# 48 list entries of each block fetched as single rows by SP and ScalarE beside the gathers of GpSimd

## The chip, the cores and the metric

The kernel runs on one core of a Trainium2 chip. The time is the device time of one execution in microseconds; a run's time is set against the median of three runs of the kernel before.

## The reference, cut to what matters

A graph layer with 50,000 nodes of 128 float32 numbers and 1,650,000 edges, sorted by destination; 50,000 of them lead from a node to itself.

```python
Xs = X[src]
m_data = Xs @ W_data.T + b_data
m_ctrl = Xs @ W_control.T + b_control
msg = jnp.where((edge_types == 0)[:, None], m_data, m_ctrl)
agg = jax.ops.segment_sum(msg, dst, num_segments=X.shape[0])
out = agg + (X @ W_self.T + b_self)
x = layernorm(x + relu(out))
```

## The kernel before

Since the matrices are applied after the sum, the kernel sums rows of x for each node and edge type and multiplies afterwards. The work goes by blocks of the sorted list. A block covers at most B = 124 nodes and has Q = 2 steps; a step has R = 14 chunks of P = 128 list entries. For each chunk GpSimd (POOL) issues one indirect DMA ("gather", line 507) that fetches 128 rows of x into one slice of a slot `y`; five slots (SLOTS) of 14 chunks go round. TensorE (PE) waits for a step's 14 gathers at once (line 514) and multiplies each chunk with a 0/1 matrix `oh` of 128 columns (64 nodes of a window, two edge types), which adds the rows into `acc` in PSUM (line 530). A float32 product is two matmul passes in the trace.

VectorE (DVE) makes these matrices for a block two blocks ahead (AHEAD = 2): `oh` at line 482, the counts of rows `cnt` for the bias at line 490. It adds `acc` into the running sums of a block (line 539), makes the moments of the rows and the result `o` (line 604). ScalarE (ACT) takes the square root for two blocks at a time (line 595). SP loads the list for ten blocks at a time (lines 182 and 184), windows of transposed x for eight (`xw`, its position read into registers at line 458) and stores each block's 124 rows (line 609), whose address is in a register.

An edge from a node to itself needs no gather: its row is in the transposed x that is loaded anyway. So 53 more list entries of each step (F; with LATE = 10 handed on, 63 columns) take the places of such edges in the list. `fill` (lines 363 to 392) does this on DVE up to five blocks ahead: it finds the places (`m`, line 372), puts in the new entries (`new`, `v_new`, lines 375 and 379), makes the list of row numbers `idx` that the gathers read (line 383), and finds the columns that were left out (`old`, `by`, lines 388 and 391). `columns` (lines 270 to 353) prepares ten blocks' lists.

The order on every engine is the order in which the program is written; each engine works through its own in turn and waits where a semaphore says so. The loop over blocks is in lines 662 to 726. In the middle of a block, after the first 7 products of a step, PE does a small product (line 398) for which DVE's `fill` waits (line 370). The block numbers come from these lines; the first block (and the last) take no fills ("plain"), and the last holds what remains of the list:

```python
CE = Q * SIZE
BE = CE + Q * F
NBLK = 2 + (E + LATE - CE) // BE
REST = E + LATE - CE - (NBLK - 2) * BE
```

So there are 448 blocks, 446 of them with 3,690 entries; the last has 686 entries in 6 chunks.

Of the kernel before, what the change touches and what calls it, by code (L numbers as in the profile page):

```python
# [11 lines left out]
F32 = mybir.dt.float32  # L12
BF16 = mybir.dt.bfloat16
U8 = mybir.dt.uint8
I32 = mybir.dt.int32
AF = mybir.ActivationFunctionType
ALU = mybir.AluOpType
AX = mybir.AxisListType
SP = mybir.EngineType.SP
DVE = mybir.EngineType.DVE  # L20

N = 50000
D = 128
ROW = 4 * D
E = 1650000
P = 128
# [6 lines left out]
R = 14  # L33
W = 64
Q = 2
# [3 lines left out]
F = 53  # L39
LATE = 10  # L40
FX = LATE + F
R1 = R
H = R + 1
C1 = Q * R1
SIZES = [P] * R
SIZE = sum(SIZES)
CE = Q * SIZE
BE = CE + Q * F
NBLK = 2 + (E + LATE - CE) // BE
REST = E + LATE - CE - (NBLK - 2) * BE  # L50
REST_ROWS = [min(n, max(0, REST - q * SIZE - sum(SIZES[:r]))) for q in range(Q) for r, n in enumerate(SIZES)]
# [2 lines left out]
GB = 10  # L54
GROUPS = -(-NBLK // GB)
GC = GB * C1
AHEAD = 2
SLOTS = 5
RAHEAD = 5
LOOP = 2048.0  # L60
COLS = 256
# [24 lines left out]
def plain(b):  # L86

    return b == 0 or b >= NBLK - 1
# [3 lines left out]
    return bass.AP(tensor=ap.tensor, offset=ap.offset, ap=[[0, n], *ap.ap])  # L92


def straight(ctx, tc, c, x, x_t, edges_t, edges_f, dst_first, first_p, out):

# [13 lines left out]
    eds = ctx.enter_context(tc.tile_pool(name="eds", bufs=2))  # L112
    ohp = ctx.enter_context(tc.tile_pool(name="ohp", bufs=AHEAD + 1))
    gat = ctx.enter_context(tc.tile_pool(name="gat", bufs=SLOTS))
    fil = ctx.enter_context(tc.tile_pool(name="fil", bufs=2))
    stp = ctx.enter_context(tc.tile_pool(name="stp", bufs=3))
    ps = ctx.enter_context(tc.tile_pool(name="ps", bufs=2, space=bass.MemoryType.PSUM))
# [59 lines left out]
    nc.vector.memset(stats, 0.0)  # L177
    most = keep.tile([P, GROUPS], F32, name="most")

    def load_edges(g):  # L180
        t = eds.tile([P, 3, GB, C1], I32, name="sdt", bufs=1)
        nc.sync.dma_start(t.rearrange("p m b c -> p (m b c)"), edges_t[:, g * 3 * GC:(g + 1) * 3 * GC])
        f = eds.tile([GB, 3, Q * FX], I32, name="sdt_f", bufs=1)
        nc.sync.dma_start(f.rearrange("b m f -> b (m f)"), edges_f[g * GB:(g + 1) * GB, :])
        loads[g] = {n: t[:, m] for m, n in enumerate("sdt")} | {n + "f": f[:, m] for m, n in enumerate("sdt")}


# [82 lines left out]
    def columns(g):  # L270

        a = loads.pop(g)
        first = begin[:, g * GB:(g + 1) * GB, :]
        steps = "p b (q r) -> p b q r"

# [87 lines left out]
    def fill(b):  # L363

        if plain(b):
            return
        g, i = divmod(b, GB)
        two = lists[b % 2]
        vf, cb = two[:, :Q * FX], two[:, Q * FX:]
        nc.vector.tensor_copy(cb, cb_g[g][:, i, :])  # L370
        m = fil.tile([P, C1, FX], F32, name="m", bufs=1)
        nc.vector.tensor_tensor(m, rk_g[g][:, i, :, None].to_broadcast([P, C1, FX]),  # L372
                                rank_no_ps[:, None, :].to_broadcast([P, C1, FX]), op=ALU.is_equal)
        new = fil.tile([P, C1, FX], F32, name="new", bufs=1)
        nc.vector.tensor_tensor(new.rearrange("p (q r) f -> p q r f", r=R1), m.rearrange("p (q r) f -> p q r f", r=R1),  # L375
                                vf.rearrange("p (q f) -> p q f", f=FX)[:, :, None, :].to_broadcast([P, Q, R1, FX]),
                                op=ALU.mult)
        v = fil.tile([P, C1], F32, name="v_new")
        nc.vector.tensor_reduce(v, new, AX.X, ALU.add)  # L379
        vi = fil.tile([P, C1], I32, name="vi")  # L380
        nc.vector.tensor_tensor(vi, v, stay_g[g][:, i, :], op=ALU.add)
        idx = fil.tile([P, C1], I32, name="idx", bufs=RAHEAD + 2)
        nc.vector.tensor_single_scalar(idx, vi, COLS.bit_length() - 1, op=ALU.logical_shift_right)
        nc.vector.scalar_tensor_tensor(col_g[g][:, i, :], idx, -float(COLS), vi, op0=ALU.mult, op1=ALU.add)
        idxs[b] = idx

        old = fil.tile([P, C1, FX], F32, name="old", bufs=1)
        nc.vector.tensor_tensor(old, m, cb[:, :, None].to_broadcast([P, C1, FX]), op=ALU.mult)  # L388
        by = fil.tile([P, Q, FX], BF16, name="by")
        with nc.allow_low_precision(reason="whole numbers below 256, one of them not 0"):  # L390
            nc.vector.tensor_reduce(by, old.rearrange("p (q r) f -> p q f r", r=R1), AX.X, ALU.add)  # L391
        bys[b] = by
# [43 lines left out]
    def passes_of(b):  # L436

        of = 2 if b == NBLK - 1 else PASS
        for p in range(C // of):
            q = p * of // R  # L440
            yield q, [k for k in chunks_of(b, q) if k // of == p]
# [44 lines left out]
    def counts(b):  # L486

        cnt = ohp.tile([P, Q, 2 * W], BF16, name="cnt")
        with nc.allow_low_precision(reason="whole numbers up to R1"):
            nc.vector.tensor_reduce(cnt, ohs[b].rearrange("p (q r) w -> p q w r", r=R1), AX.X, ALU.add)  # L490
        cnts[b] = cnt
# [9 lines left out]
    def gathers(b, ks):  # L501
# [13 lines left out]
        tc.declare_fence(wait.ins, group=f"rows{b}_{ks[0]}")  # L515
        return y

    def products(b, q, ks):
        of_step = chunks_of(b, q)
        if b == NBLK - 1:  # L520
            ys[b, q] = gathers(b, ks)
        elif ks[0] == of_step[0]:
            ys[b, q] = gathers(b, of_step)
        y = ys[b, q]
        if ks[0] == 0:
            accs[b] = ps.tile([P, Q, 3, W], F32, name="acc")
        acc = accs[b][:, q]
        for k in ks:
            r = REST_ROWS[k] if b == NBLK - 1 else SIZES[k % R]
            nc.tensor.matmul(acc[:, :2, :].rearrange("p t w -> p (t w)"), y[:r, k % R, :], ohs[b][:r, column(k), :],  # L530
                             start=k == of_step[0], stop=k == of_step[-1])
        if ks[-1] == of_step[-1] and q == steps_of(b)[-1]:
            for t in range(2):
                nc.tensor.matmul(accs[b][:, :q + 1, 2, :], to_row[:, t, :], cnts[b][:, :q + 1, t * W:(t + 1) * W],  # L534
                                 start=t == 0, stop=t == 1)
# [121 lines left out]
    for b in range(1, AHEAD):  # L657
        onehot(b)
        counts(b)
    made, fresh = 2, [2]  # L660
    ready = []
    for b in range(NBLK):
        if b == NBLK - 2:
            find_bad()
        if b == NBLK - 1:
            if pair(b - 2):
                store(pair(b - 2))
                ready.extend(pair(b - 2))
            while ready:
                store_rows(ready.pop(0))  # L670
        if b + 3 < NBLK:
            window(b + 3)
        g, i = divmod(b, GB)
        if i == 0 and g + 1 < GROUPS:
            load_edges(g + 1)
        due, fresh = fresh, range(made + 1, min(b + RAHEAD, made + (2 if b > GB // 2 else 1), NBLK - 1) + 1)
        made += len(fresh)
        for f in fresh:
            spread(f)
        if b > 0:  # L680
            add_all(b - 1)
        begin_sums(b)
        if b == NBLK - 1:
            layer(b - 1)
            moments(b - 1)
            root(pair(b - 1))
            own_part(b)
            store(pair(b - 1))
            for done in pair(b - 1):
                store_rows(done)  # L690
            for step, ks in passes_of(b):
                if ks:
                    products(b, step, ks)
            break
        if b + AHEAD < NBLK:
            onehot(b + AHEAD)
            counts(b + AHEAD)
        for q, (step, ks) in enumerate(passes_of(b)):
            if ks:
                products(b, step, ks)  # L700
            if q == 0:
                for f in due:
                    left_out_columns(f)
                for f in fresh:
                    fill(f)
            if q == 1 and b > 0:
                layer(b - 1)
            if q == 1:
                left_out_numbers(b + 1)
            if q == 1 and b > 0:  # L710
                moments(b - 1)
            if q == 1:
                for f in due:
                    left_out_matrix(f)
            if q == 1 and b + 1 < NBLK:
                positions(b + 1)
                left_out_rows(b + 1)
            if q == 2 and i == GB // 2 - 1 and g + 1 < GROUPS:
                columns(g + 1)
            if q == 1 and b > 1 and pair(b - 2):  # L720
                store(pair(b - 2))
                ready.extend(pair(b - 2))
            if q == 3 and b > 0 and pair(b - 1):
                root(pair(b - 1))
            if q == 3 and ready:
                store_rows(ready.pop(0))
# [231 lines left out]
def gnn_resnorm(  # L958
# [3 lines left out]
    x_t: bass.AP,  # L962
    edges_t: bass.AP,
    edges_f: bass.AP,
    dst_first: bass.AP,
    first_p: bass.AP,
    src: bass.AP,
# [34 lines left out]
             b_data=b_data, b_ctrl=b_ctrl, b_self=b_self)  # L1002

    with ExitStack() as own:
        straight(own, tc, c, x, x_t, edges_t, edges_f, dst_first, first_p, out)
    found = nc.values_load(bad, min_val=0, max_val=4 * P,
                           skip_runtime_bounds_check_because="a count of at most 3 * P + 2")
    with tc.If(found > 0):  # L1008
# [55 lines left out]
```

## Time and profile before

| | |
|---|---|
| median of 3 runs | 15663.81 us (15662.4 to 15665.03) |
| profiled execution | 15668.22 us |
| its span, from the first to the last instruction | 15666.5 us |
| mean granted TensorE clock | 0.664 |
| packets of the DMA engines | 474784, 905.35 MB |

In the profile's groups of instructions a row gives line, engine, operation, the tiles written and read, shapes, the count, then the busy time with the mean of one in ns, and the idle time of the engine just before them with what ended it. In the waits a row gives engine, tile and line, what it waited for, the total in us, how often and the longest. A timeline row gives start, length, engine, line and operation. A row of one line's or tile's instructions gives the least, median and greatest length in ns, and the first and last start in us. A row of windows gives the busy times (and counts) of PE, PE's weight loads, DVE, ACT and POOL, then the clock, the DMA share and GB/s. "POOLq", "SPq" and the like are the sequencers of the engines, which issue DMAs and wait for semaphores. A row of queues gives packets, MB and the share of the time of 16 DMA engines.

### The profile page before, as it was taken

The page shows a single profiled execution, that of the slowest core. Times are in us where ns is not written, and L with a number is a line of the kernel's source. Part 1 is how long each engine was busy: PE and PEld are TensorE (multiplying, and loading weights), DVE is VectorE, ACT ScalarE, POOL GpSimd, SP SyncE. Part 2 cuts the span into 40 slices and gives each one's busy share as a digit, 9 for nine tenths or more (in the row PEclk, how much of TensorE's full clock was granted, in tenths as well). Part 3 has the DMA queues.
Part 4 walks back from the last instruction along what each step waited for, and adds up shares of the span by engine and source line. Part 5 has one row for each costly group of instructions (what it writes and reads, how often), then busy time and mean ns, then how long its engine had stood idle before and what let it go on. Part 6 is the DMA issues. An engine that isn't in the chain of part 4 may idle for free. (4 is left out here: it accounts for less than half of the span.)

```text
span 15666.5 us, 97614 instructions
## 1 busy us (share of the span) xinstructions
PE 5887.6 (38%) x32436; PEld 5492.1 (35%) x32437; DVE 11899.2 (76%) x12418; ACT 69.8 (0%) x231; POOL 11833.4 (76%) x12532
## 2 busy tenths in 40 slices
PE   3333333333333333333333333333333333333333
PEld 3333333333333333333333333333333333333333
DVE  9777777777777777777777777777777777777775
ACT  0000000000000000000000000000000000000000
POOL 7777777777777777777777777777777777777777
PEclk7666666666666666666666666666666666666666
DMA  2222222222222222222222222222222222222222
GB/s 61 59 57 58 57 57 59 57 60 57 57 58 57 59 57 57 59 58 59 57 57 58 57 59 57 58 58 57 58 57 57 58 57 60 57 57 58 57 59 53
DMA packets 474784, 905.35 MB, mean 58 GB/s; under 512 B 204474, under 2 KB 260873, under 8 KB 474271
## 3 DMA queue, kind: packets, MB, share of 16 engines
q0 software_dynamic: 400736, 821.40, 20.7%
q1 hardware_dynamic: 73096, 77.42, 1.7%
q8 instruction: 260, 4.26, 0.1%
q14 instruction: 254, 2.07, 0.0%
q10 hardware_dynamic: 438, 0.20, 0.0%
HBM read 869.76 MB, written 28.44 MB: 57 GB/s over the span
## 5 line engine op out<-in xcount | busy, mean ns | idle before, releaser
L507 POOL DMA_INDIRECT y<-in_x,idx x12516 | 11826.0, 945 | 3813.9 <-issue 3811.3
L530 PE MATMUL acc<-oh,y 128*128 128x128 f32 x25044 | 4965.0, 384 | 9493.2 <-PEq L514 9493.2
L530 PEld LDWEIGHTS acc<-oh,y 128*128 128x128 f32 x25044 | 4754.9, 293 | 9816.0 <-issue 5313.4
L490 DVE TENSOR_REDUCE cnt<-oh 128x256 bf16<-128x3584 f32 x448 | 2763.2, 6168 | 15.4
L482 DVE TENSOR_TENSOR oh<-col,small 128x3584 f32<-128x3584 f32 x448 | 1736.7, 3877 | 0.0
L539 DVE TENSOR_TENSOR sums<-acc,sums 128x192 f32 x895 | 319.7, 357 | 1768.7 <-PE acc L534 1749.8
L391 DVE TENSOR_REDUCE by<-old 128x126 bf16<-128x1764 f32 x446 | 1466.4, 3288 | 15.5
L370 DVE COPY small<-cb 128x28 f32<-128x28 f32 x446 | 84.1, 189 | 1547.8 <-PE small L398 1547.8
L372 DVE TENSOR_TENSOR m<-rk,small 128x1764 f32<-128x1764 f32 x446 | 888.4, 1992 | 15.2
L375 DVE TENSOR_TENSOR new<-m,small 128x1764 f32<-128x1764 f32 x446 | 888.2, 1992 | 15.2
L379 DVE TENSOR_REDUCE v_new<-new 128x28 f32<-128x1764 f32 x446 | 887.9, 1991 | 15.2
L388 DVE TENSOR_TENSOR old<-m,small 128x1764 f32<-128x1764 f32 x446 | 884.6, 1984 | 0.0
L569 PE MATMUL po<-wmsgT,sums 128*124 128x128 f32 x1792 | 315.5, 299 | 0.0
L559 PE MATMUL po<-own_w,xT 128*124 128x256 f32 x896 | 269.4, 382 | 0.8 <-DVE h L575 0.8
L555 DVE TENSOR_TENSOR sums<-pl,sums 128x372 f32<-128x372 f32 x446 | 243.2, 545 | 16.3
L569 PEld LDWEIGHTS po<-wmsgT,sums 128*124 128x124 f32 x1792 | 229.5, 187 | 54.8 <-issue 0.8
L423 DVE TENSOR_TENSOR pl<-pl,xT 128x248 f32<-128x248 f32 x446 | 189.4, 425 | 50.4 <-DVE xT L476 5.1
L567 PE MATMUL po<-bias,sums 3*124 3x128 f32 x896 | 215.1, 319 | 0.8 <-DVE sums L539 0.8
L567 PEld LDWEIGHTS po<-bias,sums 3*124 3x124 f32 x896 | 128.9, 180 | 152.1 <-issue 150.8
L406 DVE TENSOR_SCALAR z<-node_no,at 126x256 bf16<-126x256 f32 x446 | 161.0, 361 | 15.9
L361 PE MATMUL small<-v_f,row_of 74*128 74x126 bf16 x446 | 98.8, 222 | 177.7 <-DVE at L405 128.4
L476 DVE COPY xT<-xw 128x124 f32 x448 | 104.5, 233 | 79.5 <-issue 75.5
(144 smaller groups left out, 2727.9 us busy)
## 6 DMA issues: line engine op xcount, KB each, us to landing
y<-in_x,idx POOLq DMA_INDIRECT x12516
xw<-in_x_t SPq DMA_DIRECT2D x56, 496.0 KB
out<-o SPq DMA_DIRECT2D x448, 62.0 KB
sdt<-in_edges_t SPq DMA_DIRECT2D x45, 420.0 KB
sdt_f<-in_edges_f SPq DMA_DIRECT2D x45, 14.8 KB
first_i<-in_dst_first SPq DMA_DIRECT2D x1, 450.0 KB
y<-in_x,sdt POOLq DMA_INDIRECT x6
w_all<-in_L_gnn_W_data ACTq DMA_DIRECT2D x1, 64.0 KB
```

The costliest lines, as they stand in the source:

```text
L372: nc.vector.tensor_tensor(m, rk_g[g][:, i, :, None].to_broadcast([P, C1, FX]), rank_no_ps[:, None, :].to_broadcast([P, C1, FX]), op=ALU.is ...
L375: nc.vector.tensor_tensor(new.rearrange("p (q r) f -> p q r f", r=R1), m.rearrange("p (q r) f -> p q r f", r=R1), vf.rearrange("p (q f) -> ...
L379: nc.vector.tensor_reduce(v, new, AX.X, ALU.add)
L388: nc.vector.tensor_tensor(old, m, cb[:, :, None].to_broadcast([P, C1, FX]), op=ALU.mult)
L391: nc.vector.tensor_reduce(by, old.rearrange("p (q r) f -> p q f r", r=R1), AX.X, ALU.add)
L482: nc.vector.tensor_tensor(oh, col_g[g][:, i, :, None].to_broadcast([P, C1, 2 * W]), num_ps[:, None, :].to_broadcast([P, C1, 2 * W]), op=AL ...
L490: nc.vector.tensor_reduce(cnt, ohs[b].rearrange("p (q r) w -> p q w r", r=R1), AX.X, ALU.add)
L507: copy = nc.gpsimd.indirect_dma_start(out=y[:r, k % R, :].bitcast(U8), out_offset=None, in_=x_rows, in_offset=bass.IndirectOffsetOnAxis(ap ...
L530: nc.tensor.matmul(acc[:, :2, :].rearrange("p t w -> p (t w)"), y[:r, k % R, :], ohs[b][:r, column(k), :], start=k == of_step[0], stop=k = ...
L539: nc.vector.tensor_tensor(part, accs[b][:, q], part, op=ALU.add)
L567: nc.tensor.matmul(po, a[0:3, 2, :B], bias, start=False, stop=False)
L569: nc.tensor.matmul(po, a[:, t, :B], c["wmsgT"][:, t * D:(t + 1) * D], start=False, stop=t == 1)
```

## The change

Each step of a middle block takes S = 24 more entries of the list. They are no part of a gather. `load_edges` loads their numbers into a tile of 20 x 24 for ten blocks, `offsets` turns these into byte offsets on DVE, and `single_rows(b + 2)` loads 24 of them into registers and issues 24 DMAs of one row (512 bytes) each into a tile `y1` of 24 x 128: for the first step of a block on SP, for the second on ACT. Six such tiles (ALONE) go round. After a step's 14 products PE waits for the 24 rows and adds one more product with 24 rows. The lists have 15 columns a step instead of 14 (R1), so `oh`, `m`, `new`, `old` and the other tiles that run over columns go from 28 to 30 columns; `old` takes the buffer of `new`. A middle block has 3,738 entries; there are 442 blocks.

```diff
-R1 = R
+R1 = R + 1
...
-BE = CE + Q * F
+S = 24
+LOAD = 24
+BE = CE + Q * (F + S)
...
+ALONE = 6
...
+    def offsets(g):
+        off = eds.tile([GB * Q, S], I32, name="off")
+        nc.vector.tensor_scalar(off, one_g.pop(g), float(ROW), float((N - 1) * ROW), op0=ALU.mult, op1=ALU.min)
+        off_g[g] = off
...
+        one = eds.tile([GB * Q, S], I32, name="sd1", bufs=1)
+        nc.sync.dma_start(one, edges_1[g * GB * Q:(g + 1) * GB * Q, :])
...
-        old = fil.tile([P, C1, FX], F32, name="old", bufs=1)
+        old = fil.tile([P, C1, FX], F32, name="new", bufs=1)
...
+    def single_rows(b):
+        if plain(b):
+            return
+        g, i = divmod(b, GB)
+        for q in range(Q):
+            j = alone_no[0] % ALONE
+            alone_no[0] += 1
+            y = one.tile([S, D], F32, name="y1")
+            for s0 in range(0, S, LOAD):
+                n = min(LOAD, S - s0)
+                at = i * Q + q
+                _, regs = nc.values_load_multi_w_load_instructions(
+                    off_g[g][at:at + 1, s0:s0 + n], engines=[ACT if q else SP], min_val=0, max_val=(N - 1) * ROW,
+                    skip_runtime_bounds_check_because=CLAMPED)
+                for k, r in enumerate(regs):
+                    r = nc.s_assert_within(r, 0, (N - 1) * ROW, skip_runtime_bounds_check_because=CLAMPED)
+                    copy = (nc.scalar if q else nc.sync).dma_start(y[s0 + k:s0 + k + 1, :].bitcast(U8),
+                                               x_bytes[bass.ds(r, ROW)].rearrange("(p e) -> p e", e=ROW))
+                    copy.then_inc(alone[j], 16)
...
+        if ks[-1] == of_step[-1] and not plain(b):
+            y, landed_1, n = singles.pop((b, q))
+            wait = nc.tensor.wait_ge(landed_1, n)
+            tc.declare_fence(wait.ins, group=f"single{b}_{q}")
+            nc.tensor.matmul(acc[:, :2, :].rearrange("p t w -> p (t w)"), y, ohs[b][:S, q * R1 + R, :], start=False, stop=True)
...
         if b + AHEAD < NBLK:
             onehot(b + AHEAD)
             counts(b + AHEAD)
+        if b + AHEAD < NBLK:
+            single_rows(b + AHEAD)
```

On SP, in the middle of the program before, the stores of `o` stand in a row, with the list loads (`sdt`, `sdt_f`) and the window `xw` between them:

```order
L609 DMA out<-o 124x512
L182 DMA sdt<-in_edges_t 128x840
L184 DMA sdt_f<-in_edges_f 10x378
L609 DMA out<-o 124x512 x7
L458 TENSOR_LOAD base_i
L465 DMA xw<-in_x_t 128x3968
L609 DMA out<-o 124x512 x3
```

In the changed program, at such a place (`sd` is the list of single rows, `off` their offsets):

```order
L660 DMA out<-o 124x512
L194 DMA sdt<-in_edges_t 128x900
L196 DMA sdt_f<-in_edges_f 10x378
L198 DMA sd_81022<-in_edges 20x24
L551 TENSOR_LOAD off
L556 DMA y_81032<-in_x 1x512 x24
L660 DMA out<-o 124x512
```

Ahead of each store there now stand a load of registers and 24 one-row DMAs.

ACT's whole program before, from the weights to the last square root (the second table load is for the square root):

```order
L999 ACT_TABLE_LOAD
L999 COPY wmsgT<-pw 128x128 x2
L999 COPY wselfT<-pw 128x128
L595 ACT_TABLE_LOAD
L595 ACTIVATE sd<-mv,eps 124x2 x223
L595 ACTIVATE sd<-mv,eps 124x1 x2
```

ACT's changed program, from the fourth batch of single rows on:

```order
L551 TENSOR_LOAD off
L556 DMA y_1137<-in_x 1x512 x24
L646 ACT_TABLE_LOAD
L646 ACTIVATE sd<-mv,eps 124x2
L551 TENSOR_LOAD off
L556 DMA y_1410<-in_x 1x512 x24
L551 TENSOR_LOAD off
L556 DMA y_1689<-in_x 1x512 x24
L646 ACTIVATE sd<-mv,eps 124x2
```

Between two square roots there are now two batches, one for each block.

On PE, the first step of a block before: seven products, the small one that `fill` waits for, seven more, then the layer of the block before:

```order
L361 MATMUL small<-v_f,row_of 128x126
L530 MATMUL acc<-oh,y 128x128 x7
L398 LDWEIGHTS by
L398 MATMUL small<-ones_b,by 126x1
L530 MATMUL acc<-oh,y 128x128 x7
L559 MATMUL po<-own_w,xT 124x256
```

The same place in the changed program (the `y` with a number is a tile of single rows):

```order
L377 MATMUL small<-v_f,row_of 128x126
L576 MATMUL acc<-oh,y 128x128 x7
L414 LDWEIGHTS by
L414 MATMUL small<-ones_b,by 126x1
L576 MATMUL acc<-oh,y 128x128 x7
L582 MATMUL acc<-oh,y_33911 128x128
L610 MATMUL po<-own_w,xT 124x256
```

The product with the single rows stands behind the step's last gathered chunk and ahead of the layer.

More of the change, by code (lines that the diff above doesn't have):

```diff
@@ L19 @@
 SP = mybir.EngineType.SP
+ACT = mybir.EngineType.Activation
 DVE = mybir.EngineType.DVE
@@ L92, in row_bcast, with straight @@
     return bass.AP(tensor=ap.tensor, offset=ap.offset, ap=[[0, n], *ap.ap])
-def straight(ctx, tc, c, x, x_t, edges_t, edges_f, dst_first, first_p, out):
+def straight(ctx, tc, c, x, x_t, edges_t, edges_f, edges_1, dst_first, first_p, out):
     nc = tc.nc
@@ L114, in straight @@
     gat = ctx.enter_context(tc.tile_pool(name="gat", bufs=SLOTS))
+    one = ctx.enter_context(tc.tile_pool(name="one", bufs=ALONE))
     fil = ctx.enter_context(tc.tile_pool(name="fil", bufs=2))
@@ L178, in straight @@
     most = keep.tile([P, GROUPS], F32, name="most")
+    one_g, off_g = {}, {}
+    def offsets(g):
+        off = eds.tile([GB * Q, S], I32, name="off")
+        nc.vector.tensor_scalar(off, one_g.pop(g), float(ROW), float((N - 1) * ROW), op0=ALU.mult, op1=ALU.min)
+        off_g[g] = off
     def load_edges(g):
@@ L184, in load_edges @@
         nc.sync.dma_start(f.rearrange("b m f -> b (m f)"), edges_f[g * GB:(g + 1) * GB, :])
+        one = eds.tile([GB * Q, S], I32, name="sd1", bufs=1)
+        nc.sync.dma_start(one, edges_1[g * GB * Q:(g + 1) * GB * Q, :])
+        one_g[g] = one
         loads[g] = {n: t[:, m] for m, n in enumerate("sdt")} | {n + "f": f[:, m] for m, n in enumerate("sdt")}
@@ L272, in columns @@
         a = loads.pop(g)
+        offsets(g)
         first = begin[:, g * GB:(g + 1) * GB, :]
@@ L516, in gathers @@
         return y
+    x_bytes = x.rearrange("n d -> (n d)").bitcast(U8)
+    alone = [tc.alloc_semaphore(f"alone{i}") for i in range(ALONE)]
+    got = [0] * ALONE
+    alone_no = [0]
+    singles = {}
+    def single_rows(b):
[17 more added lines that the diff above has]
+                    copy.then_inc(alone[j], 16)
+                    tc.no_tile_sem_insts.add(copy.ins.name)
+                    tc.add_to_no_dep_group(f"single{b}_{q}", copy.ins)
+            got[j] += 16 * S
+            singles[b, q] = y, alone[j], got[j]
     def products(b, q, ks):
@@ L530, in products @@
             nc.tensor.matmul(acc[:, :2, :].rearrange("p t w -> p (t w)"), y[:r, k % R, :], ohs[b][:r, column(k), :],
-                             start=k == of_step[0], stop=k == of_step[-1])
+                             start=k == of_step[0], stop=k == of_step[-1] and plain(b))
+        if ks[-1] == of_step[-1] and not plain(b):
[3 more added lines that the diff above has]
+            nc.tensor.matmul(acc[:, :2, :].rearrange("p t w -> p (t w)"), y, ohs[b][:S, q * R1 + R, :], start=False, stop=True)
         if ks[-1] == of_step[-1] and q == steps_of(b)[-1]:
@@ L659, in straight @@
         counts(b)
+    for b in range(1, AHEAD):
+        single_rows(b)
     made, fresh = 2, [2]
@@ L964, in gnn_resnorm @@
     edges_f: bass.AP,
+    edges_1: bass.AP,
     dst_first: bass.AP,
@@ L1004, in gnn_resnorm @@
     with ExitStack() as own:
-        straight(own, tc, c, x, x_t, edges_t, edges_f, dst_first, first_p, out)
+        straight(own, tc, c, x, x_t, edges_t, edges_f, edges_1, dst_first, first_p, out)
     found = nc.values_load(bad, min_val=0, max_val=4 * P,
@@ L1029 @@
         rest = a[CE:].reshape(TBL - 1, BE)
-        steps = rest.reshape(TBL - 1, Q, SIZE + F)
+        steps = rest.reshape(TBL - 1, Q, SIZE + S + F)
         cols = np.full((TBL, Q, R1, P), pad, np.int32)
@@ L1036 @@
             cols[NBLK - 1, :, r, :n] = rest[NBLK - 2, :CE].reshape(Q, SIZE)[:, at:at + n]
+        cols[1:NBLK - 1, :, R, :S] = steps[:NBLK - 2, :, SIZE:SIZE + S]
+        if k == "src":
+            arrays["edges_1"] = np.ascontiguousarray(cols[:, :, R, :S].reshape(GROUPS * GB * Q, S))
         fills = np.full((TBL * Q, FX), pad, np.int32)
-        own = steps[:NBLK - 2, :, SIZE:].reshape((NBLK - 2) * Q, F)
+        own = steps[:NBLK - 2, :, SIZE + S:].reshape((NBLK - 2) * Q, F)
         fills[Q:(NBLK - 1) * Q, LATE:] = own
@@ L1057 @@
     with tile.TileContext(nc) as tc:
-        gnn_resnorm(tc, ap["x"], ap["x_t"], ap["edges_t"], ap["edges_f"], ap["dst_first"], ap["first_p"],
+        gnn_resnorm(tc, ap["x"], ap["x_t"], ap["edges_t"], ap["edges_f"], ap["edges_1"], ap["dst_first"], ap["first_p"],
                     ap["src"], ap["dst"], ap["edge_type_2"],
```

## The prediction

> **What bounds the kernel now.** I read the busy times first, then the groups of instructions, then the waits of each engine, then the end of the timeline.
>
> ```profile
> PE 5887.6 (38%) x32436; PEld 5492.1 (35%) x32437; DVE 11899.2 (76%) x12418; ACT 69.8 (0%) x231; POOL 11833.4 (76%) x12532
> L507 POOL DMA_INDIRECT y<-in_x,idx x12516 | 11826.0, 945 | 3813.9 <-issue 3811.3
> POOL y L507 <- issue: 3813.1, 12516, 0.3
> POOL y L507 <- DMA idx<-in_edges_t: 1.1, 1, 1.1
> DVE sums L539 <- PE acc L534: 1749.8, 392, 15.2
> DVE small L370 <- PE small L398: 1547.8, 387, 4.9
> PE acc L530 <- PEq L514: 9493.2, 873, 12.8
> ```
>
> POOL and DVE both show 76%, which alone names neither. The waits do. POOL's 12,516 gathers work 11,826.0 us and stand 3,813.9 us in gaps of 0.3 us, put down to "issue", that is, to nothing that the trace shows; its largest real wait is 1.1 us, once. Work and gaps make 15,639.9 us of a span of 15,666.5 us. DVE waits for PE, and PE waits at L514, the wait for landed gathers. Everything ends behind POOL's row of gathers. The next rows are POOL's gathers in two windows, 60 to 3000 us and 6000 to 9000 us.
>
> ```profile
> L507 POOL DMA_INDIRECT y<-in_x,idx x2352 | 2225.2, 946 | 716.5 <-issue 715.3 <-DVE sums L539 0.3 <-DVE idx L383 0.3
> L507 POOL DMA_INDIRECT y<-in_x,idx x2402 | 2268.9, 945 | 731.8 <-issue 731.8
> ```
>
> In the second, a gather takes (2268.9 + 731.8) / 2402 = 1.2492 us from start to start; in the first, 1.2507 us. A block of 28 gathers lasts 28 x 1.2492 = 34.98 us. That is the time in which each other engine must do its part of a block.
>
> **What is removed.** A block holds 48 more list entries: 2 x 14 x 128 + 2 x (53 + 24) = 3,738 for 3,690. Of 1,650,010 entries (10 are padding), 3,584 are in the first block; 1,646,426 / 3,690 leaves 446 middle blocks and 686 entries, 1,646,426 / 3,738 leaves 440 and 1,706. So the last block has 14 gathers, not 6, and the program 441 x 28 + 14 = 12,362 for 12,522. Of the gathers ahead of the last block 168 go: 168 x 1.2492 = 209.9 us.
>
> **The tail gives some back.** Timeline and chain of the end:
>
> ```profile
> 15642.33 0.95 POOL L507 DMA_INDIRECT y<-in_x,sdt  x1 [0.30 <-issue]
> 15648.58 1.17 POOL L507 DMA_INDIRECT y<-in_x,sdt  x1 [0.30 <-issue]
> 15641.07 2.61 DMA y<-in_x,idx
> 15653.59 3.04 PE L530 MATMUL acc<-oh,y 128*128 128x128 f32 x12
> ```
>
> The last block's first gather starts at 15,642.33 us, and 24.2 us remain. Its six gathers are out before PE gets to them: PE is busy with the block before until 15,653.6, then takes 3.04 us for 12 matmuls (two to a chunk), and 9.9 us of closing work follow. With 14 gathers the last starts 13 x 1.249 = 16.2 us after the first and lands 2.61 us later, at 18.8; PE is by then through the earlier ones (11.3 us, then 24 matmuls at 0.25 us, 17.3) and needs 4 more, 1.0 us; with 9.87 us behind, 29.73 us. The tail costs 29.73 - 24.17 = 5.6 us more.
>
> **What is added on SP and ACT.** Each middle block adds on each of the two queues a load of 24 registers and 24 one-row DMAs. Loads of registers, one-row DMAs from ACT (the biases) and DMAs with a register address from SP are in the trace:
>
> ```profile
> L458 SPq TENSOR_LOAD <-base_i x56: 959/1110/1136, 40.9 to 15265.3; - x56
> L470 DVEq TENSOR_LOAD <-at_i x448: 337/342/591, 52.7 to 15633.5; - x150
> L609 SPq DMA_DIRECT2D out<-o x448: 253/254/316, 182.0 to 15660.6; - x150
> 2.23 0.56 ACTq L156 DMA_DIRECT2D bias<-in_L_gnn_b_data  x1
> 2.82 0.23 ACTq L156 DMA_DIRECT2D bias<-in_L_gnn_b_control  x1
> 3.09 0.26 ACTq L156 DMA_DIRECT2D bias<-in_L_gnn_b_self  x1
> SPq L609 <- DVE o L604: 14620.8, 225, 138.9
> ACT sd L595 <- DVE at L405: 15423.1, 221, 146.6
> ```
>
> Nine registers take 1.11 us on SP, four take 0.34 on DVE; 24 take at most 24/9 x 1.11 = 3.0 us. A DMA issues in 0.23 to 0.56 us. So 24 take 5.5 to 13.5 us and the whole 8.5 to 16.5 us of 34.98; I take 0.254 a row, 9.1 us, as the stores have a register address and are many. SP and ACT now wait nearly all the span, so this is cover enough. Past about (34.98 - 3.0) / 24 = 1.33 us a row it would be gone.
>
> What is queued behind: on SP the store of finished rows, the windows of x_t, and the next lists; on ACT the square root of every second block, which DVE needs a block later. The first row of a batch waits for its tile, free when PE has used the batch three blocks back, and a batch goes out two blocks ahead. For block b + 2 ACT's tile comes free as block b begins; 16.5 us later the square root of that block is not yet due, since its moments come at the end of the block. So nothing is made late, and rows have over a block to land. The list load gains one small DMA in 10 blocks, issued by SP while the lists have blocks to spare: nothing.
>
> **What is added on PE and DVE.** PE gets one more product a step, two of its matmul passes at the mean below, 0.8 us, in a wait of some 10 us a step: hidden. DVE's wide instructions go from 28 columns to 30:
>
> ```profile
> L530 PE MATMUL acc<-oh,y 128*128 128x128 f32 x25044 | 4965.0, 384 | 9493.2 <-PEq L514 9493.2
> L490 DVE TENSOR_REDUCE cnt<-oh 128x256 bf16<-128x3584 f32 x448 | 2763.2, 6168 | 15.4
> L482 DVE TENSOR_TENSOR oh<-col,small 128x3584 f32<-128x3584 f32 x448 | 1736.7, 3877 | 0.0
> L391 DVE TENSOR_REDUCE by<-old 128x126 bf16<-128x1764 f32 x446 | 1466.4, 3288 | 15.5
> L372 DVE TENSOR_TENSOR m<-rk,small 128x1764 f32<-128x1764 f32 x446 | 888.4, 1992 | 15.2
> ```
>
> One fourteenth of 6168 + 3877 + 3288 + four of about 1990 ns is 1.52 us a block (an upper bound, as part of each is fixed). DVE's two waits are (1749.8 + 1547.8) / 448 = 7.4 us a block, so 5.8 remain. Writing `old` over `new` costs nothing: the two readers and writers are DVE itself, in order. At the start DVE never rests, and there the cover is thin:
>
> ```profile
> 80.23 3.87 DVE L482 TENSOR_TENSOR oh<-col,small 128x3584 f32<-128x3584 f32 x1
> 84.18 3.34 PE L530 MATMUL acc<-oh,y 128*128 128x128 f32 x14
> 93.03 0.94 POOL L507 DMA_INDIRECT y<-in_x,idx  x1 [0.30 <-issue]
> ```
>
> The gather at 93.03 (the 71st) is the first that takes a used slot; PE frees it at 87.5, when DVE's matrix of 80.23 lets it on. By then DVE has added about 4 us (two fills 1.6, two pairs of matrix and counts 1.4, a third matrix 0.3, the columns and the offsets 0.7). 5.5 us are there; nothing to at most 4 us, once. I take nothing.
>
> Does a busier DVE slow the gathers? At the start one gather was stretched, and two windows of 350 us show what DVE's share does later:
>
> ```profile
> 9.48 1.09 DVE L199 TENSOR_TENSOR begin<-first_i,base 128x900 f32<-128x900 int32 x1
> 9.62 1.77 POOL L507 DMA_INDIRECT y<-in_x,idx  x1 [0.30 <-issue]
> 8000.00:8350.00 350.00, 131.92 (x725) 123.25 (x725) 266.78 (x277) 1.48 (x5) 264.56 (x281) 0.66 0.22 57
> 15200.00:15550.00 350.00, 133.58 (x721) 124.86 (x721) 240.87 (x257) 1.48 (x5) 264.42 (x281) 0.66 0.22 56
> ```
>
> Some instructions hold POOL back (1.77 us for 0.94), but 26 us less DVE work in a window left POOL's 281 gathers at 264.4 for 264.6 us. The wide instructions do not; of the added ones only the offsets, one of 20 x 24 in 10 blocks, may, at most 45 x 0.2 us = 9 us. I take nothing of it. The Trainium skill says in SBUF — State Buffer, SBUF: two separate sides, that DVE and GpSimd share one port pair under an exclusive lock, taken by DVE's two-port modes or by two SBUF inputs; applied to all of the added 1.52 us a block, the sum would turn into a loss of some 465 us. The stretched gather agrees with it, the two windows exclude it for the wide instructions.
>
> **What is added on the DMA engines.** The queues:
>
> ```profile
> q0 software_dynamic: 400736, 821.40, 20.7%
> q10 hardware_dynamic: 438, 0.20, 0.0%
> ```
>
> ACT's 438 packets are three weights of 128 rows with 16 more each (432) and three bias rows of 2, so a single row is one packet with data and one more, on one engine of the 16. A gather holds each engine 20.7% x 15,666.5 / 12,522 = 0.26 us. A row should cost no more: 48 x 0.26 = 12.4 us a block if all meet on one engine, beside 28 x 0.26 = 7.3 us of gathers, 20 of 34.98 us. It may delay landings, for which POOL does not wait. Nothing.
>
> **Sum.** -209.9 + 5.6 = -204.3 us. The profiled execution took 15,668.22 us around a span of 15,666.5, so 15,463.9; the median of the three runs is 4.4 us lower, 15,663.81, so 15,459.5 us: 1.3% faster.
>
> **Rivals.**
> - *The rows go one at a time.* If a queue starts a row only when the one before has landed, a row costs the 2.61 us of the landing above, well past 1.33: 24 x 2.61 + 3.0 = 65.6 us a block, 30.7 over, times 440: about 28,950 us, far slower, with PE waiting at the added product and POOL for its slots. For it: nowhere in the trace do 24 small DMAs follow each other. Against: ACT issued a bias 0.27 us behind the one before. The Trainium skill, in DMA: Bandwidth & Descriptors, Anatomy of one DMA, gives some 2 us of fixed time to a DMA but calls most of it waiting for the write's receipt, not work; as occupation it would give this rival, about as slow. The biases' 0.27 us agree with the page as far as three rows can.
> - *DVE's added work holds the gathers one for one*: +1.52 x 440 = 669 us, so 16,129 us, slower. It decides from 0.46 us a block (204 / 440). The two windows speak against it.
> - *The gathers are a little longer*, because of the extra packets or the busier DVE. At the pitch of the first window, 1.5 ns each over 12,362, 19 us are lost: 15,478 us. The gain is gone where 204 / 0.83 = 246 gathers are stretched as the one at 9.62 us was.
> - *The wider blocks leave the window of 64 nodes* and the general path runs. In the reference's lists the widest offset is 61, by counting; I leave it out.
>
> **How the numbers follow.** Hidden as summed: 0.82. Gathers a little longer: 0.08; more of the gain lost, but faster still: 0.03; all of it: 0.01. One at a time: 0.04. DVE one for one: 0.02. This gives 0.93 for faster by over 0.2% (31 us, about what can be told from no change), 0.01 for within, 0.06 for slower. The range: at the low end the tail costs nothing, 15,454, less 4 us for the spread of runs; at the high end start (4), offsets (9) and pitch (19) add up to 15,491.
>
> **What would show it.** After: 12,362 gathers, 12,348 on `idx`, at 945 ns with 0.3 us gaps and no waits of POOL; DVE near 80%; 24 rows in 6 to 14 us on SP and ACT; some 21,000 more packets on each of their queues; no wait of PE at the added product. It is wrong if POOL waits for a slot or PE for a single row, if a row takes over 1.33 us on its queue, or if the mean gather grows past 948 ns.

## The result and the profile after

The changed kernel takes 15,490.83 us (median of 4 runs, 15,489.71 to 15,491.71) against 15,663.1 us for the kernel before on the same chip: a ratio of 0.989 [0.9873, 0.9907], 172.3 us or 1.1% faster. Forecast were 15,459.5 us in a range of 15,450 to 15,491. The sign, the mechanism and the bound were as forecast; 31 us of the gain did not come.

The page of the changed kernel: busy times, ACT's DMA queue, and the groups that answer to those of before.

```profile
PE 6310.5 (41%) x33786; PEld 5706.8 (37%) x33787; DVE 12439.8 (80%) x12322; ACT 68.9 (0%) x228; POOL 11704.8 (76%) x12372
q10 hardware_dynamic: 21558, 5.65, 0.2%
...
L523 POOL DMA_INDIRECT y<-in_x,idx x12348 | 11690.2, 947 | 3766.1 <-issue 3717.4
L506 DVE TENSOR_REDUCE cnt<-oh 128x256 bf16<-128x3840 f32 x442 | 2917.9, 6602 | 15.1
L498 DVE TENSOR_TENSOR oh<-col,small 128x3840 f32<-128x3840 f32 x442 | 1831.8, 4144 | 0.0
L407 DVE TENSOR_REDUCE by<-new 128x126 bf16<-128x1890 f32 x440 | 1540.2, 3501 | 15.0
L582 PE MATMUL acc<-oh,y 24*128 24x128 f32 x1760 | 427.8, 323 | 0.0
```

POOL has 168 gathers fewer, as counted, and still stands in gaps of 0.3 us only. DVE has grown from 76% to 80% and is now the busier engine, but it isn't the bound: the waits of the engines say which of them is late.

```profile
POOL y L523 <- issue: 3721.1, 12203, 0.3
PE acc L576 <- PEq L530: 8815.2, 859, 13.8
DVE sums L590 <- PE acc L585: 1443.4, 361, 13.5
DVE small L386 <- PE small L414: 1149.3, 378, 5.2
SPq L660 <- DVE o L655: 9058.3, 222, 60.9
```

POOL stands in 12,203 gaps of 0.3 us at most, PE still waits for landed gathers, and DVE still has (1443.4 + 1149.3) / 440 = 5.9 us of rest a block, for 5.8 forecast. SP's wait for a finished `o` fell by 5,562 us to 9,058 us.

In the group of the gathers stands what was missed. Work and gaps make (11,690.2 + 3,766.1) / 12,348 = 1.2517 us from start to start; before it was (11,826.0 + 3,813.9) / 12,516 = 1.2496. The difference, 2.1 ns, times 12,348 is 26 us.

### The profile page after: what moved, and what is told of

The parts are those of the page before. It is cut to its first block, busy times and chain, and to the rows that moved or that the text cites. A ratio compares the mean times of both kernels' runs of the same rounds, so it can differ in the third digit from the quotient of the medians.

```text
span 15489.9 us, 144928 instructions
## 1 busy us (share of the span) xinstructions
PE 6310.5 (41%) x33786; PEld 5706.8 (37%) x33787; DVE 12439.8 (80%) x12322; ACT 68.9 (0%) x228; POOL 11704.8 (76%) x12372
## 3 DMA queue, kind: packets, MB, share of 16 engines
q10 hardware_dynamic: 21558, 5.65, 0.2%
## 5 line engine op out<-in xcount | busy, mean ns | idle before, releaser
L523 POOL DMA_INDIRECT y<-in_x,idx x12348 | 11690.2, 947 | 3766.1 <-issue 3717.4
L506 DVE TENSOR_REDUCE cnt<-oh 128x256 bf16<-128x3840 f32 x442 | 2917.9, 6602 | 15.1
L498 DVE TENSOR_TENSOR oh<-col,small 128x3840 f32<-128x3840 f32 x442 | 1831.8, 4144 | 0.0
L407 DVE TENSOR_REDUCE by<-new 128x126 bf16<-128x1890 f32 x440 | 1540.2, 3501 | 15.0
L590 DVE TENSOR_TENSOR sums<-acc,sums 128x192 f32 x883 | 315.5, 357 | 1459.2 <-PE acc L585 1443.4
L386 DVE COPY small<-cb 128x30 f32<-128x30 f32 x440 | 83.5, 190 | 1149.3 <-PE small L414 1149.3
L388 DVE TENSOR_TENSOR m<-rk,small 128x1890 f32<-128x1890 f32 x440 | 934.7, 2124 | 15.0
L391 DVE TENSOR_TENSOR new<-m,small 128x1890 f32<-128x1890 f32 x440 | 934.6, 2124 | 15.1
L395 DVE TENSOR_REDUCE v_new<-new 128x30 f32<-128x1890 f32 x440 | 933.7, 2122 | 15.1
L404 DVE TENSOR_TENSOR new<-m,small 128x1890 f32<-128x1890 f32 x440 | 931.7, 2118 | 0.0
L582 PE MATMUL acc<-oh,y 24*128 24x128 f32 x1760 | 427.8, 323 | 0.0
L582 PEld LDWEIGHTS acc<-oh,y 24*128 24x128 f32 x1760 | 259.0, 184 | 108.6 <-issue 6.3
```

Source lines behind the costliest of these rows:

```text
L498: nc.vector.tensor_tensor(oh, col_g[g][:, i, :, None].to_broadcast([P, C1, 2 * W]), num_ps[:, None, :].to_broadcast([P, C1, 2 * W]), op=AL ...
L523: copy = nc.gpsimd.indirect_dma_start(out=y[:r, k % R, :].bitcast(U8), out_offset=None, in_=x_rows, in_offset=bass.IndirectOffsetOnAxis(ap ...
```

## The experiments

Two theories stood for the 26 us. **The list preparation:** every ten blocks, in the function `columns`, DVE works through the lists of the next ten blocks, now 300 columns wide instead of 280; some of its instructions hold a gather that starts while they run, and the change made this cost more. **The rows:** 21,120 more small transfers, or the issuing of them, stretch gathers.

The trace favours the first. Counting every gather above 0.965 us, there were 92 before with 11.3 us above the usual 0.944, and 181 after with 37.2 us; 34.4 of these 37.2 us fall within a preparation. One preparation, POOL and DVE in the timeline of the changed kernel (start, duration):

```profile
8243.75 0.47 DVE L261 SCALAR_TENSOR_TENSOR nz<-sdt,ones_f 128x300 f32<-128x300 int32 x1
8243.80 1.24 POOL L523 DMA_INDIRECT y<-in_x,idx  x1 [0.30 <-issue]
...
8250.27 0.47 DVE L332 SCALAR_TENSOR_TENSOR cb<-nz,sdt 128x300 f32<-128x300 f32 x1
8250.50 1.06 POOL L523 DMA_INDIRECT y<-in_x,idx  x1 [0.30 <-issue]
...
8256.45 4.14 DVE L498 TENSOR_TENSOR oh<-col,small 128x3840 f32<-128x3840 f32 x1
8257.16 0.95 POOL L523 DMA_INDIRECT y<-in_x,idx  x1 [0.30 <-issue]
```

A gather that starts 0.05 us after `nz` takes 1.24 us, one that starts 0.23 us after `cb` takes 1.06, and one that starts within the 4.14 us of `oh` takes the usual 0.95. Each held gather is longer by what was left of DVE's instruction less some 0.12 us: 0.30 us where 0.42 us were left, 0.12 where 0.24 were left. In the kernel before, at the same preparation:

```profile
8231.08 0.95 POOL L507 DMA_INDIRECT y<-in_x,idx  x1 [0.30 <-issue]
8231.49 0.44 DVE L246 SCALAR_TENSOR_TENSOR nz<-sdt,ones_f 128x280 f32<-128x280 int32 x1
8232.32 0.50 DVE L251 SCALAR_TENSOR_TENSOR col<-nz,rel 128x280 f32<-128x280 f32 x1
8232.33 0.94 POOL L507 DMA_INDIRECT y<-in_x,idx  x1 [0.30 <-issue]
```

There `nz` runs while a gather is under way, and the next gather starts 0.01 us after `col`; neither is held.

**Is it only when the preparation begins?** If so, a delay of the preparation before should bring the loss, and one after should take it away. Both kernels got a filling of an unused tile at the head of `columns`:

```diff
 # before
+    nc.vector.memset(idle[:, :350], 0.0)
 # after
+    nc.vector.memset(idle[:, :64], 0.0)
```

> The kernel before, with one idle memset (128 x 350, about 0.38 us) on VectorE ahead of each of the 45 preparations of a list of ten blocks. Theory 'phase': a gather is stretched when its start falls inside the first part of a VectorE instruction with two SBUF inputs; in the kernel before the starts mostly miss. Moved by 0.38 us they hit: some 3 or 4 stretched gathers per ten blocks, 15 to 20 us more, 15678 to 15683 us. Theory 'rows' (the single rows or their packets stretch the gathers): nothing changes, 15663 us.

> The changed kernel, with one idle memset (128 x 64, about 0.1 us) on VectorE at the same place. Phase: the preparation begins 0.1 us later against the gathers, the two worst hits (1.24 and 1.23 us) go, the summed stretch falls from about 39 to 14 us: 15466 us. Rows: no change, 15491 us.

The shifted kernel before took 15,671.44 us (15,667.92 to 15,672.18; the kernel before there 15,666.25), ratio 1.0003 [0.9994, 1.0012]: 5 us more, which can't be told from no change, and not 15 to 20. Its trace has 16.9 us of stretching. The shifted kernel after took 15,494.10 us (0.9889 [0.9874, 0.9904]): nothing gained. In its trace one gather is now held by two instructions in turn, and the sum is no smaller, 39.6 us:

```profile
8248.45 1.47 POOL L525 DMA_INDIRECT y<-in_x,idx  x1 [0.30 <-issue]
```

A shift changes which gathers are held, but neither shift brought or took away the loss as expected. So the moment at which the preparation begins doesn't settle the loss by itself.

**Is it the rows?** One fixed transfer of 24 rows a step takes the place of the register load and the 24 rows (it leaves out the list's row numbers, so each step adds the same 24 rows):

```diff
-   _, regs = nc.values_load_multi_w_load_instructions(off_g[g][at:at + 1, s0:s0 + n], ...)
-   for k, r in enumerate(regs):
-       copy = (nc.scalar if q else nc.sync).dma_start(y[s0 + k:s0 + k + 1, :].bitcast(U8), x_bytes[bass.ds(r, ROW)]...)
+   copy = (nc.scalar if q else nc.sync).dma_start(y.bitcast(U8), x.bitcast(U8)[:S, :])
```

> The changed kernel with the 24 single-row DMAs of a step replaced by one DMA of 24 fixed rows on the same queue, without the load of registers (so the single rows that it adds are the wrong ones). 42,240 packets become far fewer. Phase: within 4 us of 15491, since the rows were hidden and VectorE's work is as before. Rows: the 26 us of stretched gathers go, about 15465 us.

It took 15,494.31 us (15,493.73 to 15,494.79), ratio 0.9889 [0.9874, 0.9904], with 173 stretched gathers that cost 39.5 us. Taking the single rows away gives nothing back: neither they nor the register loads are what stretches the gathers.

**Is it the width of the lists, without any rows?** The kernel before, with 30 instead of 28 columns a step in DVE's work and the tile that `old` shares, but the same 12,522 gathers, no rows and no offsets:

```diff
-R1 = R
+R1 = R + 1
...
-        old = fil.tile([P, C1, FX], F32, name="old", bufs=1)
+        old = fil.tile([P, C1, FX], F32, name="new", bufs=1)
```

> VectorE's part of the change alone once more (30 columns, the two added ones empty, 12,522 gathers, no single rows, no offsets), on a chip that runs the kernel before at its usual time. If the longer preparation of ten blocks drags the gathers: their time over 0.96 us sums to some 30 us instead of 11, and the run is about 18 us over the kernel before. If the offsets alone did it: 11 us in the trace, and no difference to the kernel before.

It took 15,690.29 us (11 runs, 15,688.78 to 15,693.65; the kernel before 15,663.71), ratio 1.0017 [1.0008, 1.0026]: 26.6 us slower, where 18 were expected. Its group of gathers and its timeline:

```profile
L507 POOL DMA_INDIRECT y<-in_x,idx x12516 | 11849.9, 947 | 3815.2 <-issue 3774.9 <-DVE cnt L490 23.2 <-DVE oh L482 12.2
```

```profile
8243.71 0.47 DVE L246 SCALAR_TENSOR_TENSOR nz<-sdt,ones_f 128x300 f32<-128x300 int32 x1
8243.76 1.23 POOL L507 DMA_INDIRECT y<-in_x,idx  x1 [0.30 <-issue]
```

945 ns a gather have become 947, with 193 stretched ones costing 38.8 us (36.9 of them within preparations), as in the changed kernel, and the gather behind `nz` stretches as it does there. The wider lists alone cost what the prediction lacked.

**What in the preparation holds a gather?** Two kernels add to the changed one, at the end of `columns`, the same eight additions of 128 x 300 numbers into an unused tile. In one both inputs lie in SBUF; in the other the second lies in PSUM.

```diff
+    for _ in range(8):
+        nc.vector.tensor_tensor(idle, v, stay, op=ALU.add)                    # two inputs in SBUF
 or
+        nc.vector.tensor_tensor(idle, v, rank.rearrange(...), op=ALU.add)     # rank lies in PSUM
```

> The changed kernel with the 8 idle additions of two SBUF inputs again, on a chip that runs the kernel before at its usual time. Hold: 3.0 us of such instructions cover 2.4 gather starts per ten blocks at 0.13 to 0.25 us each: 13 to 26 us over the changed kernel, 15505 to 15518 us, with more gathers over 0.96 us and their mean near 948.5 ns. Busy: the same in the next run.

> The same 8 additions with one input in PSUM. Hold: nothing beyond the changed kernel, 15488 to 15496 us. Busy: as the run with two SBUF inputs.

Measured: 15,527.05 us (0.9914 [0.9901, 0.9928]) with both in SBUF, 15,493.17 us (0.9892 [0.9877, 0.9908]) with one in PSUM. The profiled execution of each was its first and 24 to 27 us longer than its median, so the medians are compared. (In both profiled executions gathers that aren't stretched stand 1.2506 us apart instead of 1.2486, which over 12,362 gathers is 25 us.) The other runs are 15,524.91 to 15,529.12 and 15,492.80 to 15,493.50, 34 us apart. Their traces differ by 32.1 us in the gathers; the groups of gathers, first with two inputs in SBUF, then with one:

```profile
L526 POOL DMA_INDIRECT y<-in_x,idx x12348 | 11745.8, 951 | 3769.7 <-issue 3734.1 <-DVE cnt L509 23.5 <-PEq L533 4.6
```

```profile
L526 POOL DMA_INDIRECT y<-in_x,idx x12348 | 11713.7, 949 | 3770.6 <-issue 3734.5
```

DVE takes as long for either set of eight, 4.00 and 3.96 us. In the timelines, again in this order, all three gathers that start during the additions are held, and none:

```profile
8287.26 4.00 DVE L369 TENSOR_TENSOR idle<-v,stay 128x300 f32<-128x300 f32 x8
8287.85 1.21 POOL L526 DMA_INDIRECT y<-in_x,idx  x1 [0.30 <-issue]
8289.36 1.21 POOL L526 DMA_INDIRECT y<-in_x,idx  x1 [0.30 <-issue]
8290.88 1.21 POOL L526 DMA_INDIRECT y<-in_x,idx  x1 [0.30 <-issue]
```

```profile
8271.71 3.96 DVE L369 TENSOR_TENSOR idle<-v,rank 128x300 f32<-128x300 f32 x8
8272.41 0.95 POOL L526 DMA_INDIRECT y<-in_x,idx  x1 [0.30 <-issue]
8273.66 0.95 POOL L526 DMA_INDIRECT y<-in_x,idx  x1 [0.30 <-issue]
8274.91 0.94 POOL L526 DMA_INDIRECT y<-in_x,idx  x1 [0.30 <-issue]
```

45 preparations with three gathers held 0.27 us each make 36 us, near the 34 measured; the expectation of 15,505 to 15,518 was too small, that of the other kernel right. What holds a gather here is an instruction with two inputs in SBUF. The Trainium skill, SBUF — State Buffer, SBUF: two separate sides, says of such an instruction that against a GpSimd operation which reads SBUF it takes the shared port pair for its whole length, and that the other then blocks; these two kernels agree with it, by 34 us.

**How far do the rows carry?** 72 and 96 rows a step instead of 24:

```diff
-S = 24
+S = 72        # or 96
```

> The changed kernel with 72 single rows a step instead of 24: 12,053 gathers instead of 12,362. At 0.257 us a row and 1.8 us a load of 24 registers SP and ACT need 24 us of a block's 35. Hidden: 308 gathers of the middle blocks less, 385 us, about 1 us less tail: 15105 us, up to 20 us either way by phase. If the rows had a cost that grows with their number and was 26 us at 24 rows, 52 us of the gain would be lost: 15157 us.

> 96 single rows a step, on a chip that runs the kernel before at its usual time. From the run with 72 rows: 96 x 0.257 + 4 x 1.8 = 31.9 us of a block's 35 on each queue. Hidden: 140 gathers of the middle blocks fewer than with 72 rows, 175 us: about 14928 us. If the queue is the bound (fetching its longer program adds 3 us or more a block): over 35 us a block, at 36 us 15300 us, at 40 us 17000 us.

With 72, 15,102.92 us (15,099.49 to 15,103.77), 0.9639 [0.9626, 0.9653]: 3.6% faster than the kernel before, faster than the changed kernel, and near the 15,105 us expected if the rows are hidden. With 96, 17,696.59 us, 1.13 [1.1284, 1.1315]: slower by 13%. SP's wait for a finished `o`, which was 9,058 us with 24 rows, shows the cover running out with 72:

```profile
SPq L660 <- DVE o L655: 2217.9, 212, 64.7
```

With 72 the whole batch takes 27.6 us of SP's time, with 96 there is a batch every 40 us; SP's timelines of the two:

```profile
8030.43 27.60 SPq L556 DMA_DIRECT2D y<-in_x  x72
```

```profile
8026.17 37.95 SPq L556 DMA_DIRECT2D y<-in_x  x96
8066.50 39.69 SPq L556 DMA_DIRECT2D y<-in_x  x96
```

A block of 28 gathers lasts 35 us; the queue, not POOL, then sets the time, and the chain of work that ended last names ACT's queue:

```profile
ACTq 67%; issue 14%; DVE 9%; SPq 7%; PE 1%; DMA 1%; ACT 0%; DVEq 0%; PEldq 0%
```

I had expected 96 rows to be just hidden: 0.257 us a row and four loads make 31.9 us. The rows take 37.95 to 39.69 us, three of the loads included, so 0.34 to 0.36 us each: the instructions don't follow each other without a gap.

**Four runs that tell little.** The two kernels with added additions, the one with wide lists and the one with 96 rows first ran on a chip on which the kernel before itself took 17,787.44 us (17,784.78 to 17,789.97).

> The changed kernel with 8 idle VectorE additions (128 x 300, both inputs in SBUF, 3.0 us together) at the end of each preparation of ten blocks. Theory 'hold': a gather that starts while such an instruction runs waits for its end. 3.0 us cover 2.4 gather starts, 0.13 to 0.25 us each: 0.3 to 0.6 us in 44 preparations, 13 to 26 us more than the changed kernel, 15505 to 15518 us. Theory 'busy' (any VectorE work in that place stretches gathers): the same here, and the same in the next run.

> The same 8 additions with one input in PSUM instead of SBUF. Hold: no gather is held by them: 15492 us, as the changed kernel. Busy: 13 to 26 us more, like the run with both inputs in SBUF.

> The kernel before with lists of 30 columns instead of 28 (the two added ones empty) and `old` in the buffer of `new`: VectorE's part of the change alone, no single rows, no offsets, 12,522 gathers. Hold: the preparation of ten blocks gets longer by about 0.4 us and drags the gathers with it: some 0.4 us in 44 preparations, 15 to 22 us more than the kernel before, about 15682 us. If the single rows or the offsets stretch the gathers: as the kernel before, 15663 us.

> 96 single rows a step, 11,904 gathers. At 0.257 us a row and four loads of 1.8 us a batch takes 31.9 us of a block's 35 on SP and on ACT, which is near the end of the cover. Hidden: 140 gathers of the middle blocks fewer than with 72 rows, 175 us: about 14930 us. If SP or ACT becomes the bound (its store, window and square root come on top, or a row costs more than 0.28 us): a block takes over 35 us and the time rises, at 0.02 us a row more by 840 us.

Ratios there: 1.0028 [1.0017, 1.0039], 1.0028 [1.0017, 1.004], 1.0001 [0.9992, 1.001] and 1.5161 [1.5141, 1.5182]. POOL's waits in the kernel with wide lists show why the first three say nothing of held gathers:

```profile
POOL y L507 <- issue: 3681.7, 12075, 0.3
POOL y L507 <- remote: 1544.6, 314, 9.4
POOL y L507 <- PE acc L530: 570.8, 115, 5.1
```

POOL waited for slots there, over 2,000 us, so held gathers cost 2.8 us by the medians instead of 26.6: they came out of a wait. Both kernels with additions came out 48 to 51 us above the kernel before, whatever their inputs, though their traces differ as elsewhere: 110 gathers are held by the additions with two inputs in SBUF, by 28.0 us together, and none by those with one in PSUM. With 96 rows, where some 14,930 us were expected, the run took 26,972.91 us and single row issues lasted up to 1.4 us. Why that chip ran this program 14% longer isn't settled; the runs of the same four kernels further up are from chips with the usual time.

## Why the prediction was right, and what it missed

What bounds the kernel, what is removed and what is hidden were forecast rightly. That the time fell into the range was luck: 15,490.83 us lies 0.2 us below its upper end, and of the three terms that made up this end neither the start (the 71st gather goes out at 92.8 us for 93.0) nor the offsets (no gather starts in any of the 45) cost anything, and the third, 19 us for slightly longer gathers, stood in for a loss of 26 us that the sum had no term for.

- **Gathers removed, -209.9 us: right.** 12,348 on `idx` and 14 in the last block, 168 fewer ahead of it. Gathers that aren't stretched stand 1.2486 us apart in both kernels, so no drift of all gathers hides in the 26 us.
- **The tail, +5.6 us: right in kind, 1.5 us short.** From the last block's first gather to the end:

```profile
15458.72 0.94 POOL L523 DMA_INDIRECT y<-in_x,sdt  x1 [0.31 <-issue]
15474.94 0.91 POOL L523 DMA_INDIRECT y<-in_x,sdt  x1 [0.30 <-POOLq L1064]
15477.38 1.52 PE L576 MATMUL acc<-oh,y 128*128 128x128 f32 x4 [0.97 <-PEq L530]
```

  31.2 us to the span's end at 15,489.9, for 29.73 forecast. The gathers took 16.2 us as forecast; the last four products took 1.52 instead of 1.0, and what follows the products 1.2 us more than the 9.87.
- **Rows on SP and ACT hidden: right.** The rows' line on ACT, the register load's on SP (count: least, median and longest ns, first and last start), and a batch on each queue:

```profile
L556 ACTq DMA_DIRECT2D y<-in_x x10560: 227/228/550, 15.2 to 15368.2; - x200
L551 SPq TENSOR_LOAD <-off x440: 1419/1789/2055, 44.2 to 15348.1; - x147
```

```profile
8001.13 7.67 SPq L556 DMA_DIRECT2D y<-in_x  x24
```

```profile
8003.42 8.11 ACTq L556 DMA_DIRECT2D y<-in_x  x24
```

  With its load a batch takes 9.5 to 9.9 us, for 9.1 taken and 8.5 to 16.5 allowed. The load is cheaper than its bound of 3.0 us; a row is dearer, 7.67 / 24 = 0.32 us on SP and 0.34 on ACT for 0.254, since a move of an address (29 ns) and gaps lie between. The fixed transfer in place of the rows changed nothing, which shows them hidden. The rival of rows one at a time, at 2.6 us each, fell at once.
- **PE and DVE: right.** DVE's wide instructions grew within their bound (6168 to 6602, 3877 to 4144, 3288 to 3501 ns), PE's added product doesn't wait, and ACT's queue shows 21,558 - 438 = 21,120 packets more: two for each of 10,560 rows.
- **"Does a busier DVE slow the gathers?": the step that was mis-sized.** I wrote that wide instructions do not hold POOL and took nothing for the offsets, with at most 9 us. The first part was right: `oh` and those of `fill` that read `small` have an input in PSUM, and the counts and the other sums have only one input. But the change also widens the lists, and the instructions of the preparation, with two inputs in SBUF, go from 280 to 300 columns. The sum had no term for them. It is 26 us by the trace and 26.6 us alone on the chip. -204.3 + 26.6 + 1.5 makes -176.2; the two spans differ by 176.6.

  Most of this seems to come not from the added length but from where the gathers start. At the same instruction, before and after:

```profile
8241.11 0.94 POOL L507 DMA_INDIRECT y<-in_x,idx  x1 [0.30 <-issue]
8241.33 0.44 DVE L348 TENSOR_TENSOR rk<-rk,late 128x280 f32<-128x280 f32 x1
```

```profile
8254.33 0.46 DVE L364 TENSOR_TENSOR rk<-rk,late 128x300 f32<-128x300 f32 x1
8254.37 1.23 POOL L523 DMA_INDIRECT y<-in_x,idx  x1 [0.30 <-issue]
```

  This `rk` holds 7 gathers before (1.5 us together) and 35 after (10.0 us); `nz` holds 2 (0.4 us) and 24 (6.7 us). If starts fell evenly, the eleven such wide instructions of a preparation would cost about 17 us in 45 preparations with 280 columns and 18 with 300: an estimate from their lengths (0.43 to 0.50 us, 0.45 to 0.47) and the rule of the last section. By that estimate the kernel before, with 11.3 us, was well placed and the changed one, with 37.2, badly; with 72 rows a step and the same 300 columns it is 25.5.
- The two windows of 350 us that served as evidence mixed work that holds with work that doesn't, since a preparation comes once in ten blocks. What could have shown it stood in the kernel before: sort the gathers by their length and see what DVE does as each long one starts.
- The rival "the gathers are a little longer" came true in kind, at 2.1 ns instead of 1.5, by neither of the causes as I had put them. I had given it 0.08. The other 3.5 us of the 31 lie in the medians: the profiled execution before was 4.4 us above its median, the one after 0.9.

## What to carry to other kernels

Where an engine's gathers bound the kernel, single rows from SP's and ScalarE's idle queues take load off it at 0.32 to 0.34 us a row (24 rows in a batch) plus a register load, until the batch outgrows the time of a block; count what the queue really takes for a row, gaps included, since past that point the loss is steep (0.9639 with 72 rows, 1.13 with 96). When a change widens another engine's work, cost not only that engine's time but each instruction that can hold the bound engine: those with two inputs in SBUF, by their number and length, wherever a gather can start in them. Put it down as a range and not as one value: for much the same preparation it was 11 to 40 us here, by where the gathers happened to start. An input that lies in PSUM anyway keeps an instruction out of the way.

## What the runs showed of the hardware that I had not expected

- How long a gather is held follows one rule. In the ten traces from chips with the usual time, 1,459 gathers start at least 0.04 us into a wide DVE instruction of a preparation (or an added addition) with two inputs in SBUF, and have more than 0.14 us of it before them; 1,457 of them are longer than usual by what is left less 0.12 us, to within 0.02 us. The most for one instruction is about 0.3 us (1.24 us for 0.94; 1.47 when two such instructions held it in turn). A gather under way isn't touched; of 127 that start in the first 0.03 us of the instruction all but three aren't either, nor is one that starts beside an instruction with one input in PSUM.
- The second input need not be wide. `z` (one tile and `at`, one number a partition, both in SBUF) holds gathers too, 10 of them by 1.1 us together in the changed kernel, and 74 by 8.4 us on the chip with 17,787 us in the kernel with one input in PSUM.
- What such holds cost isn't set by the moment at which the preparation begins alone: 11.3 us of stretching in the kernel before, 16.9 in the same shifted, 38.8 with 30 columns. That the longer way from `h_loop` to the last `rk`, 10.95 us for 10.24 at the place shown, and the gathers held on it bring the next starts into the next instructions is argued, not shown; why the kernel before is so well placed is open.
- The price of a row on a queue isn't its issue time. 228 ns of issue and 29 ns of address became 0.32 to 0.34 us with 24 and 0.34 to 0.36 with 96 rows a batch, and on one chip single issues lasted 1.4 us. The packets of the queue that brings instructions grew with the rows (q14: 595 in the changed kernel, 1,237 with 72 rows). That the gaps are waits for these packets is a guess that no run here tests.
